# Where DVE adds the kept shared-expert output to the residual in a mixture-of-experts layer

## The chip, the cores and the metric

The kernel runs on one core of a Trainium2 chip. The metric is the time of one launch in device microseconds; smaller is better. Times given here are a median of several runs, and a profile is one execution of its own, recorded by the hardware.

## The reference, cut to what matters

The reference is a stack of four layers on x of 4 sequences x 1024 tokens x 128 features, in float32. Each layer has an attention-like part and a feed-forward part, with a layer norm behind each. The change lies in the feed-forward part of the last layer, a mixture of 32 experts of width 128, of which each token uses 4, and a shared expert of width 512 that every token uses:

```python
def _L3_ffn_ref(x, ...):
    flat = x.reshape(B * T, D)
    scores = softmax(flat @ router_w.T + router_bias)
    topk_scores, topk_idx = top_k(scores, 4)
    topk_scores = topk_scores / clip(topk_scores.sum(-1), 1e-12)
    h = silu(einsum('nd,ehd->neh', flat, gate_w)) * einsum('nd,ehd->neh', flat, up_w)
    expert_out = einsum('neh,edh->ned', h, down_w)
    sel = take_along_axis(expert_out, topk_idx[:, :, None], axis=1)
    out = (sel * topk_scores[:, :, None]).sum(axis=1)
    out = out + silu(flat @ sgate_w.T) * (flat @ sup_w.T) @ sdown_w.T
    return out.reshape(B, T, D)
...
x = layernorm(x + _L3_attn_ref(x, ...))
x = layernorm(x + _L3_ffn_ref(x, ...))
```

The layer's first part, `_L3_attn_ref`, forms u and v (256 wide) from the normalised rows, mixes v between tokens with a Toeplitz matrix per head, multiplies by u and projects back to 128.

## The kernel before

The residual x stays in SBUF for the whole kernel, as 32 tiles of 128 tokens x 128 features. Layer 3 takes the tokens in three parts: a (the first half, 16 tiles), b and c (a quarter each, 8 tiles, so 128 x 1024 numbers). Each part passes these steps:

- `l3_attn` (L1561): the attention-like part. For each of two halves of the width PE and ACT make v and u (L1626, L1580), and DVE mixes v with the Toeplitz weights and multiplies by u (L1637, L1639, L1643; 4 + 12 + 4 instructions a half).
- `l3_route`: the router; DVE selects four experts of each token and computes for each (token, choice) its place in a list sorted by expert, `posl3b` for part b.
- `spread`: POOL scatters the rows of x with indirect DMAs into that list in DRAM, `l3rb`, 8 x 4 = 32 DMAs of 128 rows (L1301).
- `l3_shared` (L1686): the shared expert. PE, ACT (L739) and DVE (`hs`, L740) make it; for parts b and c the result is not added at once but kept by ACT in an SBUF tile `sh`, since the spread still reads x as it was.
- `small_experts` (L1718), called for this layer by `l3_experts`: SP loads the list in groups of 512 rows (`xg`, L1332), PE transposes them (`tp`, copied to `xgT` by ACT, L167), multiplies by the gate and up weights of the experts (`gu`, L157), ACT applies silu (`sg`, L1748), DVE multiplies (`hg`, L1749), PE turns that round and DVE copies it out (`hT`, L169), PE multiplies by the down weights, ACT copies the result (`yg`), and SP writes it to a second list in DRAM, `l3yb`. In step g the code emits `up(g + 1)`, `turn(g)` (the one with `hT`), `inputs(g + 2)` and `down(g - 1)`; the last step, g == ng, holds only the last `down`, and then `rest_of`, an If for lists that are longer than expected, which is not taken here.
- `collect` (L1381): POOL gathers the rows back (`yt`, L1301), and DVE adds each with its weight to x (L1392). There are eight buffers for `yt`, so POOL's later gathers wait for DVE's adds.
- `finish` or `close`: the last norm (L192 to L209) and SP's DMAs to the output (`out_x`, L1808).

`all` weaves these together. A generator `on` holds the side work in order: part b's spread and part a's collect and finish abreast of part c's `l3_attn` and route, then c's spread, then b's collect and finish. `mix` lets the side work advance beside the main work (shared expert and experts of b, then of c) by the estimated durations that the steps yield. The order on each engine is then settled when the program is built: a planner takes the instructions by estimated times, within their dependencies, and an instruction may so be placed far from where it is written. `queued` is what ties side work down: every instruction that the side generator emits gets an ordering edge (without a semaphore) behind the last instruction that the main work has emitted on the same engine, which `self.latest` holds.

The line of this change stands in the loop over b and c:

```python
self.run(self.mix(self.l3_experts(p, wall3), on, 0.75, p is c))
s = slice(p.t0, p.t0 + QT)
self.nc.vector.tensor_tensor(self.x[:, s, :], sh, self.x[:, s, :], ALU.add)
```

It is written behind the experts (L1962), and does not go through `queued`, so it has its data dependencies alone: `sh` must be there, and the part's spread must have read x.

Of the kernel before, what the change touches and what calls it, by code (L numbers as in the profile page):

```python
# [15 lines left out]
ALU = mybir.AluOpType  # L16
# [14 lines left out]
QT = NT // NQT  # L31
# [11 lines left out]
E3, F3, K3 = 32, 128, 4  # L43
# [31 lines left out]
class Kernel:  # L75
# [1585 lines left out]
    def l3_route(self, part):  # L1661
        nc = self.nc
        with ExitStack() as ctx:
# [15 lines left out]
            yield from self.positions(cp, "l3" + part.name, mask, w, part.nt, E3, K3)  # L1679
            yield (10.0,)  # L1680

    def mark(self, name):
        self.listed.add(name)
        yield (0.0,)
# [30 lines left out]
        cp = self.pool(ctx, "l1fw")  # L1715
        return self.load(cp, self.ins["l1_w"])

    def small_experts(self, lay, ne, part, wall):  # L1718

        nc = self.nc  # L1720
        pos, wk, ids, done, used = self.route[lay + part.name]
        rows, ys, total = self.lists[lay, part.name]
        tl = self.likely(part, ne, K3)
        with ExitStack() as ctx:
            gp = self.pool(ctx, lay + "fg" + part.name, 3)
            ps = self.pool(ctx, lay + "fpe" + part.name, 2, space=PSUM)
            ng = tl // 4
            xgTs, ess, hs, hTs = {}, {}, {}, {}

            def inputs(g):  # L1730
                xg = self.gathered(gp, rows, g, done, part.nt * K3)
                xgTs[g] = self.tile(gp, [P, BLK], "xgT")
                self.transposes(ps, xgTs[g], [xg[:, i, :] for i in range(4)], on_act=True, tag="tp")

            def up(g):
                es = ess[g] = self.experts_of(ids, g, ne)
                xgT = xgTs.pop(g)
                h = hs[g] = self.tile(gp, [P, 4, P], "hg")
                for c in range(2):
                    pg = self.tile(ps, [P, 2, 2, P], "gu")  # L1740
                    for i in range(2):
                        self.mm(
                            pg[:, i].rearrange("p a f -> p (a f)"),
                            xgT[:, (2 * c + i) * P : (2 * c + i + 1) * P],
                            wall[:, bass.ds(es[2 * c + i] * (3 * P), 2 * P)],
                        )
                    sg = self.tile(gp, [P, 2, P], "sg")
                    nc.scalar.activation(sg, pg[:, :, 0, :], AF.Silu)  # L1748
                    nc.vector.tensor_tensor(h[:, 2 * c : 2 * c + 2, :], sg, pg[:, :, 1, :], ALU.mult)  # L1749

            def turn(g):
                h = hs.pop(g)
                hT = hTs[g] = self.tile(gp, [P, BLK], "hT")
                self.transposes(ps, hT, [h[:, i, :] for i in range(4)], on_act=False, tag="tp")

            def down(g):
                es, hT = ess.pop(g), hTs.pop(g)
                py = self.tile(ps, [P, 4, D], "yp")
                for i in range(4):
                    pm = self.mm(py[:, i, :], hT[:, i * P : (i + 1) * P], wall[:, bass.ds(es[i] * (3 * P) + 2 * P, P)])  # L1760
                yg = self.tile(gp, [P, 4, D], "yg")
                if lay == "l3" or g % 2:
                    nc.scalar.copy(yg, py)
                    marks = (pm,)
                else:
                    marks = (pm, nc.vector.tensor_copy(yg, py))
                nc.sync.dma_start(
                    out=ys[g * 4 * P : (g + 1) * 4 * P, :].rearrange("(t p) d -> p t d", p=P), in_=yg
                )
                return marks  # L1770

            def rest(g):
                inputs(g)
                up(g)
                turn(g)
                down(g)


            inputs(0)
            inputs(1)  # L1780
            up(0)
            for g in range(ng + 1):
                if g + 1 < ng:
                    up(g + 1)
                if g < ng:
                    turn(g)
                if g + 2 < ng:
                    inputs(g + 2)
                marks = down(g - 1) if g else ()
                if g == ng:  # L1790
                    self.rest_of(used, tl, total, rest)
                    self.listed.add(f"made {lay}{part.name}")
                yield (3.7, *marks)
# [1 line left out]
    def l1_experts(self, part, wall):  # L1795
        return self.small_experts("l1", E1, part, wall)

    def l3_experts(self, part, wall):
        return self.small_experts("l3", E3, part, wall)

    def finish(self, part):

# [84 lines left out]
    def all(self):  # L1887
        a, rest = self.first, self.rest
        b, c = rest
        r = self.both[1]  # L1890
        a2, m2, n2 = self.by_rows
        with ExitStack() as ctx:
            lgp = self.pool(ctx, "l2lg")
            self.l2_lg = self.tile(lgp, [P, NT, E2], "lg")
            with ExitStack() as early:
# [13 lines left out]
                with ExitStack() as c2:  # L1909
                    wall = self.l1_wall(c2)  # L1910
# [4 lines left out]
            with ExitStack() as c2:  # L1915
                wall = self.l1_wall(c2)
# [6 lines left out]
            on = self.served(  # L1923
                self.chain(self.rows_in(a2), self.onward(a, True)),
                (lambda: self.rows_done >= B + 2, self.routed(m2)),
                (lambda: self.rows_done == 2 * B, self.routed(n2)),
            )
            self.run(self.mix(self.l2_attn(1), on, drain=False))
            with ExitStack() as c3:
                with ExitStack() as c2:  # L1930
                    wall = self.l2_wall(c2)
                    self.press(on, listed("l2m"))
                    self.run(self.mix(self.l2_experts(m2, wall), on, drain=False))
                    self.press(on, lambda: {"l2n", "routed l3a"} <= self.listed)
                    sw, wall3 = self.l3_wall(c3, True)
                    on = self.chain(on, self.rows_in(m2))
                    self.run(self.mix(self.l2_experts(n2, wall), on, drain=False))
                self.press(on, listed("l3a"))
                yp = self.pool(c3, "l3y", 8)

                on = self.chain(
                    on, self.collect("l2", n2, K2, yp, which=(0, 1, 4, 5)),
                    self.abreast(
                        self.chain(self.l3_attn(b), self.mark("mixed l3b"), self.l3_route(b)),
                        self.collect("l2", n2, K2, yp, which=(2, 3, 6, 7)),
                    ),
                    self.abreast(
                        self.chain(self.spread("l3", b, K3), self.when(listed("made l3a")), self.last(a, yp)),
                        self.chain(self.l3_attn(c), self.mark("mixed l3c"), self.l3_route(c)),
                    ),  # L1950
                    self.spread("l3", c, K3), self.when(listed("made l3b")), self.last(b, yp),
                )
                self.run(self.mix(self.chain(self.l3_shared(a, sw), self.l3_experts(a, wall3)), on, 0.75, False))
                hold = self.pool(c3, "l3hold", 2)
                for p in (b, c):
                    self.press(on, listed("mixed l3" + p.name))
                    sh = self.tile(hold, [P, QT, D], "sh")
                    self.run(self.mix(self.l3_shared(p, sw, sh), on, 0.75, False))
                    self.press(on, listed("l3" + p.name))
                    self.run(self.mix(self.l3_experts(p, wall3), on, 0.75, p is c))  # L1960
                    s = slice(p.t0, p.t0 + QT)
                    self.nc.vector.tensor_tensor(self.x[:, s, :], sh, self.x[:, s, :], ALU.add)  # L1962
                self.run(self.close(c, yp))
        bad = self.nc.values_load(self.flag[0:1, 0:1], min_val=0, max_val=1)
        with self.tc.If(bad > 0):
            with ExitStack() as ctx:
# [9 lines left out]
                for p in self.parts:  # L1976
                    self.run(self.onward(p))
                    with ExitStack() as c2:
                        sw, wall = self.l3_wall(c2)
# [167 lines left out]
```

## Time and profile before

| | |
|---|---|
| time, median of 3 runs | 2411.06 us (2410.7 to 2413.85) |
| profiled execution | 2413.21 us, of it 2411.4 us span |
| mean granted TensorE clock | 0.818 of full speed |
| busy: PE, DVE, ACT, POOL | 1616.9, 1263.6, 825.0, 722.6 us |
| part b: spread on POOL | 2047.03 to 2088.3 us |
| part b: experts on PE, first and last `hT` on DVE | 2092.67 us on; 2121.99 and 2194.61 us |
| part c: spread on POOL | 2225.00 to 2270.3 us |
| part c: last `hT` on DVE | 2350.97 us |
| part c: gathers on POOL | 2357.50 to 2386 us |
| the adds of `sh` (L1962) | 2 x 1.226 us, at 2089.66 and 2271.62 us |

Times in the profile are microseconds from the start of the span. A line of a timeline gives the start, the duration, engine, line of the code, operation, output <- inputs, how many instructions are put together, and in brackets the engine's idle time just before, with what ended it. `DMA l3rb<-x,posl3b` is the scatter of part b, `yt<-l3ya,posl3a` a gather of part a. "issue" is time in which the engine waited for nothing that the profile shows.

### The profile page before, as it was taken

To read this page: it belongs to the slowest core of one execution; us is meant where nothing else is said; L and a number is where in the kernel's file an instruction comes from. 1 tells how busy PE (TensorE), PEld (TensorE's weight loads), DVE (VectorE), ACT (ScalarE), POOL (GpSimd) and SP (SyncE) were. 2 spreads that over 40 slices of the span, in tenths; PEclk is the share of its full clock that TensorE was granted. 3 is DMA by queue.
4 is the path that set the end of the run, shared out by engine and by line. 5 is a ranking of instruction groups with operands and counts; after the bars stand their busy time and mean duration, and the time that the engine had idled before them with its cause. 6 is when DMAs were issued, how large, how long until landed. Compare 5 with 4: busy or idle time off the path is not lost. (4 is left out here: it accounts for less than half of the span.)

```text
span 2411.4 us, 27036 instructions
## 1 busy us (share of the span) xinstructions
PE 1616.9 (67%) x9017; PEld 967.3 (40%) x9017; DVE 1263.6 (52%) x3630; ACT 825.0 (34%) x1180; POOL 722.6 (30%) x681
## 2 busy tenths in 40 slices
PE   7626876975661778487969787887745798357160
PEld 3214333853320337345623232344523486245160
DVE  8957894655570565224545675473611265236233
ACT  6701571422330333122236564642201164223030
POOL 1031484135227000435132002002272200735725
PEclk9856887988785888788979998988977899678575
DMA  9930002334101016212130000031321131222232
GB/s 309 288 112 0 20 34 90 112 115 160 62 31 53 15 34 200 83 44 74 38 106 21 1 1 16 3 114 40 143 85 35 44 112 46 76 79 62 89 89 68
DMA packets 215530, 187.10 MB, mean 78 GB/s; under 512 B 16528, under 2 KB 194064, under 8 KB 214864
## 3 DMA queue, kind: packets, MB, share of 16 engines
q1 hardware_dynamic: 194672, 142.29, 18.7%
q0 software_dynamic: 20704, 42.86, 5.8%
q8 instruction: 84, 1.38, 0.2%
q14 instruction: 70, 0.57, 0.1%
HBM read 88.49 MB, written 96.60 MB: 77 GB/s over the span
## 5 line engine op out<-in xcount | busy, mean ns | idle before, releaser
L1055 ACT ACTIVATE pr<-sc 128x1024 f32<-128x1024 f32 x288 | 279.7, 1021 | 319.9 <-PE sc L157 184.9
L157 PE MATMUL gu<-ld,xgT 128*128 x640 | 177.4, 423 | 88.8 <-issue 38.7
L157 PE MATMUL sc<-qm,kT 32*128 32x512 f32 (+3 forms) x1536 | 199.2, 558 | 13.7 <-issue 12.3
L157 PE MATMUL s<-pr,va 128*32 128x512 f32 (+3 forms) x1536 | 177.1, 528 | 46.0 <-issue 26.2
L157 PEld LDWEIGHTS gu<-ld,xgT 128*128 128x128 f32 x640 | 127.5, 210 | 119.1 <-issue 49.7
L165 PE MATMUL tp<-ld,hg 128*128 128x128 f32 x624 | 104.0, 289 | 92.1 <-ACT hT L167 38.0
L169 DVE COPY hT<-tp 128x512 f32<-128x512 f32 x118 | 81.0, 686 | 159.3 <-remote 73.9
L157 PE MATMUL gu<-wall,xgT 128*128 x304 | 156.1, 640 | 2.7 <-ACT xgT L167 2.0
L1061 DVE TENSOR_TENSOR pr<-pr,ld 128x512 f32<-128x512 f32 (+1 forms) x160 | 92.2, 581 | 100.6 <-ACT pr L1055 98.5
L165 PEld LDWEIGHTS tp<-ld,hg 128*128 128x128 f32 x624 | 81.5, 149 | 144.7 <-issue 46.9
L165 PE MATMUL tp<-ld,xg 128*128 128x128 f32 x396 | 68.9, 305 | 102.1 <-DMA xg<-l3rc 48.5
L1749 DVE TENSOR_TENSOR hg<-sg,gu 128x256 f32<-128x256 f32 x160 | 65.8, 417 | 134.9 <-ACT sg L1748 95.8
L167 ACT COPY xgT<-tp 128x512 f32<-128x512 f32 x99 | 58.0, 586 | 213.0 <-PE tp L165 91.1
L157 PEld LDWEIGHTS sc<-qm,kT 32*128 32x128 f32 x1536 | 84.8, 197 | 113.6 <-issue 77.4
L1507 ACT ACTIVATE sg<-gu 128x512 f32<-128x512 f32 x76 | 45.2, 597 | 225.7 <-PE gu L157 109.4
L1748 ACT ACTIVATE sg<-gu 128x256 f32<-128x256 f32 x160 | 61.1, 385 | 163.2 <-PE gu L157 80.9
L1301 POOL DMA_INDIRECT l1ra<-x,posl1a x64 | 93.1, 1455 | 59.5 <-DVE posl1a L1276 40.3
L157 PEld LDWEIGHTS s<-pr,va 128*32 128x32 f32 x1536 | 38.9, 113 | 156.6 <-issue 109.5
L1509 DVE TENSOR_TENSOR hg<-sg,gu 128x512 f32<-128x512 f32 x76 | 51.7, 682 | 92.1 <-ACT sg L1507 48.7
L1301 POOL DMA_INDIRECT yt<-l1yr,posl1r x64 | 60.9, 951 | 124.1 <-DVE x L1392 79.3
L165 PEld LDWEIGHTS tp<-ld,xg 128*128 128x128 f32 x396 | 52.4, 158 | 107.6 <-issue 59.0
L1301 POOL DMA_INDIRECT l1rr<-x,posl1r x64 | 61.7, 965 | 99.5 <-DVE posl1r L1276 80.3
(440 smaller groups left out, 3498.8 us busy)
## 6 DMA issues: line engine op xcount, KB each, us to landing
wall<-wall SPq DMA_DIRECT2D x16, 768.0 KB
l3ra<-zero SPq DMA_DIRECT2D x1, 6144.0 KB
ld<-in_l_w SPq DMA_DIRECT2D x2, 3072.0 KB
wall<-we SPq DMA_DIRECT2D x24, 256.0 KB
ld<-in_l_w SPq DMA_DIRECT2D x1, 6144.0 KB
l1ra<-zero SPq DMA_DIRECT2D x1, 5120.0 KB
l1rr<-zero SPq DMA_DIRECT2D x1, 5120.0 KB
xg<-l3ra SPq DMA_DIRECT2D x20, 256.0 KB
```

Of the source, the lines that this page charges most:

```text
L157: return self.nc.tensor.matmul(out, lhsT, rhs, start=start, stop=stop)
L165: nc.tensor.transpose(pt[:, k * P : (k + 1) * P], s, self.ident)
L167: nc.scalar.copy(dst, pt[:, : n * P])
L169: nc.vector.tensor_copy(dst, pt[:, : n * P])
L1055: nc.scalar.activation(pr, sc[h], AF.Exp)
L1061: nc.vector.tensor_tensor(d, d, cst["tril"].unsqueeze(1).unsqueeze(1).to_broadcast([P, 2, n, P]), ALU.mult)
L1301: ins = self.nc.gpsimd.indirect_dma_start(**kw)
L1507: nc.scalar.activation(sg, gu[:, 0, :], AF.Silu)
L1509: nc.vector.tensor_tensor(h, sg, gu[:, 1, :], ALU.mult)
L1748: nc.scalar.activation(sg, pg[:, :, 0, :], AF.Silu)
L1749: nc.vector.tensor_tensor(h[:, 2 * c : 2 * c + 2, :], sg, pg[:, :, 1, :], ALU.mult)
```

## The change

The add becomes a small generator, `held`, that is handed to the experts. In their last step, behind the last `turn` and ahead of the If, `queued` emits it, so that it gets the ordering edge behind DVE's last instruction of the main work, the last `hT` copy. The line behind the experts in `all` goes. The add itself, its operands and its duration stay the same; it is done once for b and once for c.

```diff
+    def held(self, part, sh):
+
+        s = slice(part.t0, part.t0 + part.nt)
+        self.nc.vector.tensor_tensor(self.x[:, s, :], sh, self.x[:, s, :], ALU.add)
+        yield (1.0,)
+
...
-    def small_experts(self, lay, ne, part, wall):
+    def small_experts(self, lay, ne, part, wall, held=None):
...
                 if g == ng:
+                    if held:
+                        self.queued(held)
                     self.rest_of(used, tl, total, rest)
...
-    def l3_experts(self, part, wall):
-        return self.small_experts("l3", E3, part, wall)
+    def l3_experts(self, part, wall, held=None):
+        return self.small_experts("l3", E3, part, wall, held)
...
-                    self.run(self.mix(self.l3_experts(p, wall3), on, 0.75, p is c))
-                    s = slice(p.t0, p.t0 + QT)
-                    self.nc.vector.tensor_tensor(self.x[:, s, :], sh, self.x[:, s, :], ALU.add)
+                    self.run(self.mix(self.l3_experts(p, wall3, self.held(p, sh)), on, 0.75, p is c))
```

## The prediction

> **What bounds the kernel now.** I read the page first (section 1: PE busy 67% of the span, DVE 52%, POOL 30%, so no engine carries the whole), then the one line that the change moves, then the timelines of DVE, POOL and PE around it, and last a table of busy time by stretch. The source view of L1962 gives the two adds, what DVE stood for ahead of them, and that nothing is listed as having waited for them:
>
> ```profile
> L1962 DVE TENSOR_TENSOR x<-sh,x x2: 1226/1226/1226, 2089.7 to 2271.6; 128x1024 f32<-128x1024 f32 x2
> ...
>   DMA l3rc<-x,posl3c: 33.7, 1
>   DMA l3rb<-x,posl3b: 30.5, 1
> ```
>
> So the adds do not run where the program writes them, behind the experts. They need `sh` and the end of the spread (the scatters read the rows of x that the add overwrites), and DVE takes them as soon as it may: part b's at 2089.66, part c's at 2271.62, each time ahead of the experts' first `hg`. DVE is in order, so what stands behind them waits too. DVE's timeline shows what that is for b:
>
> ```profile
> 2089.66 1.23 DVE L1962 TENSOR_TENSOR x<-sh,x 128x1024 f32<-128x1024 f32 x1 [30.54 <-DMA l3rb<-x,posl3b]
> 2090.80 0.61 DVE L1637 TENSOR_SCALAR y<-v,ld 128x256 f32<-128x256 f32 x2
> 2091.32 2.46 DVE L1639 SCALAR_TENSOR_TENSOR y<-v,ld,y 128x256 f32<-128x256 f32 x6
> ...
> 2098.75 0.42 DVE L1749 TENSOR_TENSOR hg<-sg,gu 128x256 f32<-128x256 f32 x1 [0.73 <-ACT sg L1748]
> ...
> 2120.10 0.35 DVE L1392 SCALAR_TENSOR_TENSOR x<-yt,wkl3a,x 128x128 f32<-128x128 f32 x1 [15.81 <-DMA yt<-l3ya,posl3a]
> ```
>
> Half of part c's Toeplitz mix (2090.80 to 2098.03, 7.2 us) lies behind the add, with its inputs ready since 2066.1, when ACT ended the last u. The first `hg` is not held by it: it waits for ACT's sg. And PE, ahead of both, waited for the same spread:
>
> ```profile
> 2092.67 2.01 PE L165 MATMUL tp<-ld,xg 128*128 128x128 f32 x8 [26.25 <-DMA xg<-l3rb]
> ```
>
> POOL's timeline is what sets these stretches: 32 scatters of b from 2047.03 at 1.27 us each, then at once the gathers of part a. Its indirect DMAs take about 0.95 us, but not beside the add and the Toeplitz mix, nor beside a long run of L1392:
>
> ```profile
> 2088.62 0.98 POOL L1301 DMA_INDIRECT yt<-l3ya,posl3a  x1 [0.30 <-issue]
> 2089.91 1.81 POOL L1301 DMA_INDIRECT yt<-l3ya,posl3a  x1 [0.30 <-issue]
> 2092.03 0.99 POOL L1301 DMA_INDIRECT yt<-l3ya,posl3a  x1 [0.30 <-issue]
> 2093.32 1.95 POOL L1301 DMA_INDIRECT yt<-l3ya,posl3a  x1 [0.30 <-issue]
> 2095.58 2.93 POOL L1301 DMA_INDIRECT yt<-l3ya,posl3a  x1 [0.31 <-issue]
> ...
> 2226.33 5.98 POOL L1301 DMA_INDIRECT l3rc<-x,posl3c  x1 [0.30 <-issue]
> ...
> 2271.87 1.82 POOL L1301 DMA_INDIRECT yt<-l3yb,posl3b  x1 [0.30 <-issue]
> ```
>
> The table by stretch shows the stages (the columns are PE, PEld, DVE, ACT and POOL busy, then granted clock, DMA share, GB/s): while POOL works without a break, PE hardly does, behind the spread too (12.61 of 41 us), and it is full only once the gathers have stopped.
>
> ```profile
> 2047.00:2088.00 41.00, 12.24 (x45) 6.90 (x45) 10.10 (x41) 10.66 (x19) 31.53 (x32) 0.67 0.16 59
> 2104.00:2145.00 41.00, 12.61 (x38) 8.48 (x37) 5.41 (x14) 4.88 (x9) 25.37 (x27) 0.62 0.21 56
> 2145.00:2197.00 52.00, 46.63 (x288) 41.05 (x288) 34.47 (x124) 26.76 (x52) 10.20 (x11) 0.89 0.31 91
> ```
>
> **The change, part by part.** Durations are those of the profiled execution, 2413.21 us (span 2411.4 and 1.8 around it); the median of the runs is 2411.06, so 2.15 comes off at the end.
>
> *The two stands go (30.54 and 33.70 us of DVE).* Worth nothing by themselves: the spread hides them. PE's next work waited 26.25 us for xg of the same spread, and 48.52 us in part c. If that cover were gone they would cost the whole 64 us.
>
> *The Toeplitz half moves* to about 2066, beside the scatters. Out of the gathers it takes 1.95 + 2.93 - 2 x 0.95 = 2.98 us of POOL. Beside scatters the price lies between 0 (the eight L209 at 2235.68, beside which the scatters of 2235.14 and 2236.41 stayed at 0.96) and 4.3 (32 of L1392, the same operation as L1639, cost one scatter 5.98 - 0.96 = 5.02 in 8.48 us of DVE; for 7.2 us that is 4.3). I take 2.98, the same instructions beside the same engine. So 0 for POOL's stream as a whole, with -2.98 to +1.3 as ends; the experts of b may start up to 4.3 later.
>
> *The adds leave the gathers:* -(1.81 - 0.95) - (1.82 - 0.95) = -1.73 us of POOL. Both streams then end sooner by that, and what PE gets behind them with it.
>
> The Trainium skill ("SBUF — State Buffer", section "Who interferes with whom") says that a tensor_tensor with both inputs in SBUF contends only with GpSimd's reads, and infers that writing descriptors escapes it; by that rule the adds cost POOL nothing and the sum would be 0 in place of -1.73. The two rows of 1.81 and 1.82 us speak against the rule here.
>
> *The eight L209 behind c's add* (2272.77, 2.23 us) move to about 2238, and SP's four out_x DMAs behind them to the same place, away from between the loads of xg on SP's queue. Nothing on either side (0 to -1): the third xg is used only at 2282.20.
>
> *b's add in its new place.* DVE's last hT of b ends at 2195.28; the add then takes 1.23 ahead of six L1392 and the route of c (posl3c at 2202.97). Behind that, DVE has 2.38 us idle ahead of `hs` (2205.53), waiting for PE, and POOL reaches the spread of c only at 2225.00. So 0; with that cover gone, +1.23, and POOL's gather beside it could take 0.86 more. Ends: 0 and +2.1.
>
> *c's add in its new place*, at about 2351.65 behind the last hT. Behind it wait four L1392, statistics, the DVE branch of the If (2355.9) and the L209 of part b. The last gathers start at 2357.50; the chain of waits names L209 for that, but these write b's rows, which a gather of l3yc doesn't use; SP passed the If only at 2356.8, after the last l3yc write had landed. DVE then idles 2.21 us for the first yt. So 0; if DVE does gate the gathers, +1.23.
>
> Sum: -1.73, between -5.7 and +2.9 (-1.73 with -2.98 and -1, or with +1.3, +2.1 and +1.23). 2413.21 - 1.73 - 2.15 = 2409.3.
>
> **The rivals.** *A wait that takes the place of the one removed (slower).* DVE's order is planned, and the add's place is free in it. At 2104.30 DVE already stood 15.81 us for a gather of part a (L1392), with `hg` behind it. If such an L1392 now comes ahead of the experts' first `hg` rather than behind the third, that `hg` slips from 2098.75 to about 2118. The price is at least the 5.5 us of experts' work that was done from 2098.75 to 2104.30, at most the whole 15.81 again; I take 10, which gives 2419. It decides as soon as one L1392 precedes the first `hg`. For it: this order is a matter of a microsecond in the plan. Against: the trace shows three `hg` going first.
>
> *The freed DVE time carries through (faster).* POOL stood 52.5 us in four waits for DVE's L1392 of part a (33.59, 11.24, 2.24, 5.38), and so c's spread began at 2225.00, 22.0 after posl3c was ready. If 7.2 us less DVE work among the experts of b brings those adds forward by as much, the spread and all behind it come 7.2 + 1.7 = 8.9 earlier, at most 22 + 1.7 = 23.7; I take 11, which gives 2400. Against it: DVE had time enough from 2104 to 2143, and it was PE and ACT that stood.
>
> *The add stays where it was.* The edit ties it behind the last hT on DVE, so hardly: 2411.
>
> **How the numbers follow.** 0.2% is 4.8 us, about what a measurement of this kernel can tell from no change (its runs lie 3.2 apart): faster is below 2406.2, slower above 2415.9. The sum's case: 0.42 (0.09 faster, 0.29 same, 0.04 slower, as the order elsewhere may shift a little); its own range is 2405 to 2414. The carry-through: 0.28 (0.27 and 0.01 same). The new wait: 0.27 (0.26 and 0.01 same). The add unmoved: 0.03, same. Together 0.36 faster, 0.34 same, 0.30 slower. The range runs from 2393 (half way from 2400 to its end of 2387) to 2422 (half way from 2419 to its end of 2409.3 + 15.8 = 2425), which leaves out about one in ten on each side.
>
> **What would show it.** Right: no DVE idle of 30 us ahead of an add; the Toeplitz half at about 2066 to 2073; part a's second to fifth gather at 0.95; scatters of 1 to 4 us beside the mix; both adds right behind the last hT, with DVE idle behind them. Wrong: an L1392 ahead of the first `hg`; spread c starting before 2220 or after 2230; gathers of c starting over 1 us after SP has passed the If; or the order of PE and ACT in the experts of b differing from before.

## The result, and the profile after

The changed kernel takes 2408.92 us (median of 11 runs, 2402.6 to 2417.2); the kernel before, over 11 runs, 2413.85 us (2410.1 to 2419.7). The ratio is 0.9979, with a 95% interval of 0.9964 to 0.9995: a gain of 0.05 to 0.36%, against 2409.3 us, or 0.07% below 2411.06, that were forecast. The profiled execution took 2410.17 us, with a span of 2408.4.

DVE's timeline after the change, to be read against the one shown before: the Toeplitz half now runs at 2060, as soon as the first v is there, and the adds run 2.4 and 3.5 us behind the last hT copy of their part.

```profile
2060.35 0.61 DVE L1637 TENSOR_SCALAR y<-v,ld 128x256 f32<-128x256 f32 x2 [3.10 <-issue]
...
2096.27 0.42 DVE L1755 TENSOR_TENSOR hg<-sg,gu 128x256 f32<-128x256 f32 x1 [28.49 <-ACT sg L1754]
...
2115.47 0.35 DVE L1392 SCALAR_TENSOR_TENSOR x<-yt,wkl3a,x 128x128 f32<-128x128 f32 x1 [15.59 <-DMA yt<-l3ya,posl3a]
...
2192.99 1.15 DVE L1685 TENSOR_TENSOR x<-sh,x 128x1024 f32<-128x1024 f32 x1
...
2200.11 0.69 DVE L740 TENSOR_TENSOR hs<-sg,pu 128x512 f32<-128x512 f32 x1 [1.86 <-PE pu L157]
...
2232.65 2.14 DVE L209 TENSOR_SCALAR x<-x,mv,rstd 128x128 f32<-128x128 f32 x8
...
2352.01 1.19 DVE L1685 TENSOR_TENSOR x<-sh,x 128x1024 f32<-128x1024 f32 x1
...
2356.80 0.35 DVE L1392 SCALAR_TENSOR_TENSOR x<-yt,wkl3c,x 128x128 f32<-128x128 f32 x1 [2.71 <-DMA yt<-l3yc,posl3c]
```

DVE's stand has not gone; it has only changed its name. It lasts 28.49 us and ends with ACT's sg, and the second one of 15 us, for a gather of part a, is there as before. PE waits for the same load as before:

```profile
2091.96 1.97 PE L165 MATMUL tp<-ld,xg 128*128 128x128 f32 x8 [27.38 <-DMA xg<-l3rb]
```

What changed is POOL's timeline. Scatters beside the mix are longer than 0.96 us, the first gathers of a and b are short, the gather beside the moved add of b is long (1.64 us), and one scatter of c is longer than it was (7.33 us; 5.98 before):

```profile
2061.44 1.15 POOL L1301 DMA_INDIRECT l3rb<-x,posl3b  x1 [0.30 <-issue]
...
2067.05 1.56 POOL L1301 DMA_INDIRECT l3rb<-x,posl3b  x1 [0.30 <-issue]
...
2089.14 0.97 POOL L1301 DMA_INDIRECT yt<-l3ya,posl3a  x1 [0.30 <-issue]
2090.41 0.94 POOL L1301 DMA_INDIRECT yt<-l3ya,posl3a  x1 [0.30 <-issue]
...
2193.32 1.64 POOL L1301 DMA_INDIRECT yt<-l3ya,posl3a  x1 [0.30 <-issue]
...
2219.67 7.33 POOL L1301 DMA_INDIRECT l3rc<-x,posl3c  x1 [0.31 <-issue]
...
2267.76 0.97 POOL L1301 DMA_INDIRECT yt<-l3yb,posl3b  x1 [0.30 <-issue]
```

The long scatter is not the change's doing: two later profiles of the same two kernels have it the other way round, 7.33 us before and 5.98 after. In each of these four profiles it ends about 0.86 us after DVE's run of 32 adds of part a, and either the first or the second scatter of c is the one that is caught, which moves the spread of c by 1.2 us. The longest scatter beside the mix varies in the same way, with 1.56 us here and 3.00 us in the later profile of this kernel.

The second place where something changed is SP's queue at the start of part c's experts. First before the change, then after it:

```profile
2271.67 0.92 SPq L1332 DMA_DIRECT2D xg<-l3rc  x2
2273.39 2.01 SPq L1808 DMA_DIRECT2D out_x<-x  x4
2275.45 1.77 SPq L1332 DMA_DIRECT2D xg<-l3rc  x3
```

```profile
2267.56 0.37 SPq L1332 DMA_DIRECT2D xg<-l3rc  x1
2268.02 2.18 SPq L1816 DMA_DIRECT2D out_x<-x  x4
2270.25 2.00 SPq L1332 DMA_DIRECT2D xg<-l3rc  x3
```

The four output DMAs of part a stood behind the second load of xg; now they stand behind the first, and the second load comes 2.70 us behind the first in place of 0.42. The table by stretch (part b's experts; columns as before) shows the same two regimes as before the change:

```profile
2102.00:2143.00 41.00, 10.39 (x35) 7.71 (x36) 6.16 (x15) 5.01 (x10) 23.27 (x25) 0.64 0.23 61
2143.00:2195.00 52.00, 44.10 (x285) 38.97 (x283) 35.68 (x127) 26.93 (x52) 12.49 (x12) 0.92 0.32 91
```

Put together from POOL's timelines, in us. The last two columns are the same two kernels on another chip, number 4 of the record. The experiments ran on this one and on chips 2 and 15. On these three the kernel before has medians of 2053 to 2055 us, and its runs lie between 2043 and 2063 us, apart from two slow ones on chip 4 (4570 and 8117 us):

| stage | before | after | before, chip 4 | after, chip 4 |
|---|---|---|---|---|
| spread of b | 41.3 | 42.4 | 41.2 | 43.7 |
| first 36 gathers of a | 48.7 | 44.7 | 49.7 | 46.3 |
| first scatter of b to first scatter of c | 178.0 | 174.5 | 155.0 | 153.9 |
| spread of c | 45.3 | 46.5 | 46.5 | 45.3 |
| gathers of b | 40.6 | 39.7 | 40.8 | 39.8 |
| last gather of b to first gather of c | 46.3 | 48.0 | 15.3 | 18.6 |
| first gather of c to the end | 53.9 | 54.1 | 53.9 | 53.9 |
| first scatter of b to the end | 364.4 | 363.2 | 311.7 | 311.7 |

Of the 3.0 us between the two first spans, 1.9 had arisen before the first scatter of b (2047.03 against 2045.17), where the order on PE, DVE, ACT and POOL is the same; the part that the change touches gives 1.2. (The gathers of c before the change last to 2397.3 us, not to 2386 as said above.)

### The profile page after: what moved, and what is told of

It is laid out like the page before. It is cut to its first block, busy times and chain, and to the rows that moved or that the text cites. A ratio compares the mean times of both kernels' runs of the same rounds, so it can differ in the third digit from the quotient of the medians.

```text
span 2408.4 us, 27028 instructions
## 1 busy us (share of the span) xinstructions
PE 1599.0 (66%) x9017; PEld 956.7 (40%) x9017; DVE 1262.4 (52%) x3630; ACT 822.5 (34%) x1179; POOL 720.1 (30%) x681
## 5 line engine op out<-in xcount | busy, mean ns | idle before, releaser
L157 PE MATMUL gu<-wall,xgT 128*128 x304 | 155.0, 636 | 2.7 <-ACT xgT L167 2.0
L1301 POOL DMA_INDIRECT l1ra<-x,posl1a x64 | 93.0, 1454 | 59.0 <-DVE posl1a L1276 39.8
```

Source lines behind the costliest of these rows:

```text
L157: return self.nc.tensor.matmul(out, lhsT, rhs, start=start, stop=stop)
L1301: ins = self.nc.gpsimd.indirect_dma_start(**kw)
```

## The experiments

The theory: the change works through what DVE runs beside POOL's indirect DMAs; DVE's stand itself is worth nothing; and SP's order gives back in part c what POOL saves. The rivals: the add alone hindered POOL, the order elsewhere did it, or DVE's stand cost time. Of the stages in the table, two differ between the first chip and chip 4: 23 us up to c's spread and 31 between the gathers of b and of c, much of it on the first chip in waits that its profile names "remote" (ended by something that it cannot name) and "issue". Why is not known, so the experiments are compared with one another and with the two kernels on chip 4. A profile's stages repeat better than the times, but not exactly. With c's add in the same place, the gathers of b repeat to 0.2 us. But in kernels with the same order on DVE and POOL in part b, the spread of b takes 42.4 or 43.7 us, and the 36 gathers end between 88.2 and 90.2 us from its first scatter; a difference of 1 us there between two profiles shows nothing by itself.

**Both kernels on chip 4.**

> The kernel before, unchanged, for its profile on the same chip as the next three. On the chip of the first four runs the kernel before took 2053 us and not 2411, and engines stood less for 'remote' and 'issue'. Theory: first scatter of b to the end of the first 36 gathers of a 91.3 us, as in only_c, which has the same order up to there; gathers of b 40.8; first xg load of c to the first hT of c 10.7 us, as in only_b.

> The changed kernel, unchanged, on that chip. Theory (POOL saves, SP gives back): first scatter of b to the end of the first 36 gathers 90.2 us, about 1 less than before; gathers of b 39.8, 1 less; but SP now holds four out_x DMAs between the first and the second xg load of c, so first xg load to first hT of c takes 12.7 to 15.6 us, 2 to 5 more than before. Sum within 3 us of before, so the ratio lies between 0.9985 and 1.0015. Rival (POOL alone): 10.7 us there too, and 2 us faster.

Measured: 91.25 and 90.24 us from the first scatter of b to the end of the 36 gathers, gathers of b 40.8 and 39.8, first xg load of c to first hT 11.4 and 13.6, to the last hT 48.5 and 50.7. Ratios: 0.9997 (0.9976 to 1.0017) and 0.9988 (0.9969 to 1.0006). The two savings of 1 us and the loss of over 2 are all there; neither ratio is clear of 1.

**One add at a time** (chip 2). In `all`:

```diff
-self.l3_experts(p, wall3, self.held(p, sh))
+self.l3_experts(p, wall3, self.held(p, sh) if p is b else None)   # only_b; only_c: p is c
+... behind the experts, for the other part: self.run(self.held(p, sh))
```

> Part b's add moved as in the change, part c's left where it was. Theory (POOL): the change works only through what DVE runs beside POOL's gathers. From the first scatter of b to the end of the first 36 gathers of a: 87.4 us as in the changed kernel (90.3 before); the gathers of b take 40.6 us as before (39.7 in the changed kernel). Time about 0.9 us above the changed kernel's, 1 to 3 below before. Rival (order): what the planner reorders elsewhere carries the difference; then part c alone, whose order of loads and transposes changes, carries it, and this kernel is equal to before within 1 us.

> Part c's add moved as in the change, part b's left where it was. Theory (POOL): first scatter of b to the end of the first 36 gathers of a 90.3 us as before, DVE idle 30 us ahead of the add of b; gathers of b 39.7 us as in the changed kernel; time 0 to 1 us below before. If the end of those gathers to the first gather of c still takes 48.0 us (46.3 before), c's move costs as much behind them as it saves. Rival (order): most of the gain is here, 2 us or more below before.

only_b: 90.16 us to the end of the 36 gathers (87.4 was expected from the first chip), gathers of b 40.8, first load to first hT 10.7; ratio 0.9999 (0.9976 to 1.0021). only_c: 91.25, 39.75, but 15.6 to the first hT, and 22.5 us from the gathers of b to those of c; ratio 1.0015 (0.999 to 1.0041). From the first scatter of b to the end: 311.5 and 316.3 (311.7 before). So in the profile c's move alone costs more than it brings (the ratio leaves that open), and nothing there speaks for the rival by which it would carry the gain. The gains in time that were expected, 1 to 3 us and 0 to 1 us, don't show in these ratios.

**The mix parted from the add** (chip 2). mix_first ties b's early add behind the mix; stand_kept keeps the wait, in one column's multiplication by 1, but not the add:

```diff
+add_manual_dep(add.ins, <last L1643 of the first half>, NoSync)      # mix_first
...
+e = self.x[:, p.t0 + QT - 1, 0:1]                                    # stand_kept, for b
+self.nc.vector.tensor_scalar(e, e, 1.0, None, ALU.mult)
```

> Part b's add stays ahead of the experts and waits for the spread, but is tied behind part c's first half of the Toeplitz mix; part c's add as in the change. It parts the mix from the add. Theory (POOL): the spread of b takes 42.4 us as in the changed kernel, the first 36 gathers of a 44.7 + 0.9 = 45.6 (48.7 before), their sum ends at 88.3 us from the first scatter. The stand of DVE ahead of the add is about 21 us, and hides nothing. Rival (the stand itself costs): the run ends at 90 as before.

> The changed kernel with one more DVE instruction, a multiplication by 1 of one column of the last tile of part b's x, that waits for the spread of b where the add did, ahead of the Toeplitz mix: the stand is kept, the 1.2 us of the add beside the gathers are not. Theory (POOL): DVE idle about 30 us ahead of it; the spread of b takes 41.3 us as before, the first 36 gathers of a 48.7 - 0.9 = 47.8, their end 89.4 us from the first scatter; time about 2 us above the changed kernel's. Rival (only the add hindered POOL, the mix doesn't): 87.4 us as in the changed kernel, and the same time.

POOL's timeline in mix_first, a scatter beside the mix and the gather beside the add; then DVE's stand and the gather beside the mix in stand_kept:

```profile
1760.45 3.00 POOL L1301 DMA_INDIRECT l3rb<-x,posl3b  x1 [0.31 <-issue]
...
1785.25 1.82 POOL L1301 DMA_INDIRECT yt<-l3ya,posl3a  x1 [0.30 <-issue]
```

```profile
1783.70 0.15 DVE L1970 TENSOR_SCALAR x<-x 128x1 f32<-128x1 f32 x1 [30.49 <-DMA l3rb<-x,posl3b]
```

```profile
1788.55 3.27 POOL L1301 DMA_INDIRECT yt<-l3ya,posl3a  x1 [0.30 <-issue]
```

To the end of the 36 gathers, all on chip 2: 90.10 (mix moved), 90.75 (add moved), 90.16 (both, only_b), 91.25 (neither, only_c). The spread takes 43.6 us with the mix beside it and 41.2 without. So both hinder POOL, wherever they run. What each move is worth alone these sums don't show, since 90.10 to 90.75 lies within what the stage varies by. With neither moved it ended at 91.25 both times (only_c, before_here), and with both at 88.2 to 90.2, so together they bring 1 to 3 us, though ACT's order at the start of b's experts differs between these kernels too. The whole stand of 30.49 us, put back, costs 0.35 us to the end (312.07 against 311.72 in the changed kernel on chip 4), less than such stages vary: it is hidden. Ratios 0.9992 and 1.0006, neither clear of 1. The 88.3 and 89.4 expected were too low by 1.4 to 1.8: the spread took 43.6 us and not 42.4 in mix_first, and in both kernels the second half of the mix runs beside these gathers on this chip and lengthens two or three of them (1.09 to 1.95 us).

**SP's order** (chip 15). Part a's output DMAs from ACT's queue:

```diff
-self.nc.sync.dma_start(
+(self.nc.scalar if part is self.first else self.nc.sync).dma_start(
```

> The changed kernel, but part a's eight output DMAs are issued by ACT and not by SP, so that none stands between two loads of xg; DVE and POOL keep their order, PE and ACT take the second transposes of xg ahead of the experts' first products again, as before the change. Theory (the DMAs on SP's queue give back what POOL saves in part c): the second xg load is issued 0.4 us behind the first (2.7 in the changed kernel), first load to first hT of c 10.7 to 11.5 us (13.6), from the last gather of b to the first of c 16.3 us (18.6), gathers of b stay at 39.8; from the first scatter of b to the end 309.5 us (311.7), time 1 to 3 us below the changed kernel's. Rival (the load's delay is hidden, the order of PE and ACT made the difference or nothing did): 13 us or more from first load to first hT, and the same time.

The second load comes 0.41 us behind the first, first load to first hT 12.0 (13.6 with the DMAs between the loads), last gather of b to first gather of c 16.7 (18.6), from the first scatter to the end 308.6, 3.1 below. Of these 3.1 us, 2.0 lie behind the gathers of b; the others arose ahead of c's spread, which the DMAs don't touch. The place is shown by all the kernels with eight buffers on these chips: first load to first hT takes 12.7 to 15.6 us where the DMAs stand between the loads, and 10.7 to 12.0 where they don't. Between out_on_act and the changed kernel the order on PE and ACT differs too (the second transposes of xg ahead of the first products or behind them), and no run parts that from the DMAs. The time does not show it: 0.9995 (0.9977 to 1.0013).

**What the new places have to spare** (chip 15). Three more adds of zeros behind each moved add:

> The changed kernel with three more DVE instructions of the same size behind each of the two moved adds (x plus zeros), about 3.5 us more at each place. It asks what the new places cost when they are no longer covered. Theory: in part b 1.9 us of DVE's idle time ahead of hs take half of it, the rest is seen by at most 2 us in the start of c's spread; in part c the gathers start where they did, as they don't wait for DVE, and DVE has 2.7 us idle for the first yt; from the first scatter of b to the end 311.7 to 314 us. Rival (DVE gates the spread and the gathers at both places): 7 us more, 318.7.

To the end 313.9 us (311.7), 1.0001 (0.9978 to 1.0024). In part b the extra adds are hardly seen: c's spread starts 154.2 us behind the first scatter of b (153.9). In part c only the moved add stands ahead of the If; the planner put the three extra ones behind it:

```profile
1990.24 1.19 DVE L1686 TENSOR_TENSOR x<-sh,x 128x1024 f32<-128x1024 f32 x1
...
1991.67 2.45 DVE L1688 TENSOR_TENSOR x<-zero,x 128x1024 f32<-128x1024 f32 x2
...
1994.16 1.23 DVE L1688 TENSOR_TENSOR x<-zero,x 128x1024 f32<-128x1024 f32 x1
...
1997.35 0.34 DVE L1392 SCALAR_TENSOR_TENSOR x<-yt,wkl3c,x 128x128 f32<-128x128 f32 x1
```

The first gather started at 1992.72, while DVE was still adding, so these gathers don't wait for DVE's work behind the If, though the chain of waits names it (L209). What they do wait for is in the traces: in all fourteen profiles the first gather of c starts 0.97 us after the last write to `l3yc` has landed (1991.75 and 1992.72 here, 2356.53 and 2357.50 before the change, 2353.26 and 2354.23 after it). In out_on_act and stand_kept the moved add ended 0.1 us after that landing, and the gather was no later. More DVE work ahead of the If was not tried. Of the 2.2 us to the end, 1.1 arose ahead of the adds of c (first load to first hT 14.7 us against 13.6); in part c the norm behind the extra adds held the first add of gathered rows to 1997.35, 1.8 us after its yt had landed.

**Dense DVE work beside the scatters** (chip 4). The largest hindrance in these traces is neither add nor mix, but the last 32 adds of part a, 8.5 us without a gap beside c's first scatters. In spaced and spaced_b the order on every engine stays that of the changed kernel and of only_b, and those adds only wait:

```diff
+behind = done[len(done) - 3 if n == 0 else len(done) - 1]   # 2nd or 4th scatter of c's tile
+add_manual_dep(<first L1392 of the tile>, behind, Sync)
```

> The changed kernel with its instructions in the same order on every engine, but the last 32 adds of part a (L1392), which DVE ran without a gap beside the first scatters of c, now wait in groups of four for the second and the fourth scatter of each of c's first four tiles. Theory (dense DVE work holds POOL): the spread of c takes 41.2 to 42.5 us in place of 46.5, and all behind it comes about 4 us earlier, time 2 to 5 us below the changed kernel's. Rival (the long scatter has another cause, the start of the spread itself): 46.5 us and the same time.

> As the last, but only part b's add is moved; part c's stays where it was before the change. Theory: the spread of c 41.2 to 42.5 us, first xg load to first hT of c 10.7 us since the out_x DMAs stay behind the second load, gathers of b 40.8; 1 to 4 us below the last kernel, 4 to 8 below before. Rival (the order of SP doesn't matter): 12.7 us or more there, and 1 us above the last kernel for the slower gathers.

```profile
1906.53 1.92 DVE L1903 SCALAR_TENSOR_TENSOR x<-yt,wkl3a,x 128x128 f32<-128x128 f32 x7 [2.19 <-DMA l3rc<-x,posl3c]
```

With such gaps, at most seven adds in a row, no scatter of c takes over 1.01 us, and the spread takes 40.4 us in place of 45.3 to 46.5. To the end: 307.5 and 305.5 us (311.7). Times 2047.23 and 2045.34 us; ratios to the kernel before 0.9975 (0.9955 to 0.9995) and 0.9962 (0.9941 to 0.9984). spaced_b, with c's add left early, has its first hT 11.5 us behind the first load, spaced 14.1.

**More buffers for yt** (chip 15), sixteen in place of eight on top of spaced_b; yt16_act adds c's move and the output DMAs on ACT:

```diff
-yp = self.pool(c3, "l3y", 8)
+yp = self.pool(c3, "l3y", 16)
```

> spaced_b with sixteen buffers for yt in place of eight, so that POOL gathers the whole of part a without a wait for DVE's adds; all 64 adds of a then wait for scatters of c, four at a time. Theory (what starts c's spread is POOL's stand for DVE's adds of part a, and not the route, which is ready 18 us sooner): c's spread starts when posl3c is ready, about 136 us from the first scatter of b (154 in spaced_b), and from the first scatter of b to the end it takes 288 to 292 us (305.5); time 12 to 18 us below spaced_b. Rival (something else in c, the shared expert or the experts of b, holds the start): 300 us or more.

> The last kernel with the change in full (part c's add moved too) and part a's output DMAs on ACT. Theory: gathers of b 39.8 us where the last has 40.6, no DMA between the loads of xg; within 2 us of the last kernel, as ACT now waits for part a's norm ahead of some of its copies. Rival (ACT is held by these DMAs): 3 us or more above the last kernel.

yt16_b takes 2019.22 us, a ratio of 0.9833 (0.9802 to 0.9865); yt16_act 2026.56 us, 0.9863 (0.9835 to 0.9892). The second is 7 us behind in time, as its rival said, but in the profile's stages level (282.4 us to the end in yt16_b, 281.3 in yt16_act). The profile of yt16_b is of an execution of 2031.42 us, 12 us above its median, so that stays unsettled. yt16_b moved more than expected, and the expectation named but half of the cause. DVE's timeline at the start of b's experts, in spaced_b and then in yt16_b:

```profile
1813.50 0.35 DVE L1397 SCALAR_TENSOR_TENSOR x<-yt,wkl3a,x 128x128 f32<-128x128 f32 x1 [17.09 <-DMA yt<-l3ya,posl3a]
```

```profile
1801.58 0.42 DVE L1763 TENSOR_TENSOR hg<-sg,gu 128x256 f32<-128x256 f32 x1 [0.78 <-ACT sg L1762]
1801.92 0.68 DVE L169 COPY hT<-tp 128x512 f32<-128x512 f32 x1
```

With eight buffers an add of part a stands among the first `hg` and waits 17 us for its gather; with sixteen all these adds come later, and the first hT of b is there 54.7 us after the first scatter, not 73.4. POOL also gathers without a stand, and c's spread starts at 123.9 us (154.0), as soon as POOL has done the 64 gathers; posl3c was ready 10 us sooner. What each of the two is worth alone, no run shows. First load to first hT of c gives 6 us back (17.4 against 11.5).

## Why the prediction was right

*The stands are worth nothing*: right, by stand_kept. *The new places are covered*: right, for b by heavy and in the trace (1.86 us idle behind the add, ahead of hs), for c by the trace, where the last write to `l3yc` and not DVE releases the gathers (2.71 us idle behind the add). The add of b holds a gather in its new place too, 1.64 us in place of 0.95; POOL's next stand, 4.24 us in place of 5.38, hides that. The adds do not stand right behind the last hT, as was said, but 2.4 and 3.5 us behind it.

*The Toeplitz mix*: mis-sized. Out of the gathers it took about 3 us, as said; beside the scatters it cost 1.1 us in some profiles (the first chip's, out_on_act and the two with sixteen buffers) and 2.4 in the others, in place of 2.98, so the move brought a gain of its own. It started at 2060 and not at 2066, since it needs v first and u last. *The add of b*, 0.86: one gather was longer by 0.87 where the add stood, but what was left of that behind the 36 gathers, 0.5 us by stand_kept and nothing by mix_first against only_b, is less than the stage varies by. *The add of c*, 0.87: 0.9 and 1.0.

*The L209 and SP's DMAs behind c's add*, "nothing on either side (0 to -1)": wrong, in sign. L209 went to 2232, but the DMAs did not move with it into the spread: on SP's queue they stand behind the first load of xg and were issued at 2268.02, though their rows were ready at 2234.8; so they moved ahead of the second load. That is 1.6 to 2.0 us by out_on_act, together with the order of PE and ACT that goes with it, and eats the saving of part c.

*The sum* of -1.73 thus came out as -1.2 on the first chip and 0.0 on chip 4, with the mix's gain left out and one term of the wrong sign. In both, c's long scatter, which falls either way without the change, has its part: +1.2 on the first chip, -1.2 on chip 4. Without it the stages give about -2.4 and +1.2, so even the sign is not settled by them. The measured ratio of 0.9979 and chip 4's 0.9988 (0.9969 to 1.0006) both leave room for the sum; that the median fell by 4.9 is more than the stages show, and the rest was not traced to the change. That 2408.92 lies 0.4 us from the 2409.3 forecast is luck: the forecast started from 2411.06, the median of three runs, while eleven runs of the same kernel gave 2413.85.

The Trainium skill ("SBUF — State Buffer", section "Who interferes with whom") infers that a tensor_tensor doesn't hinder the writing of descriptors. In mix_first, where nothing else ran on DVE beside it, the add still made one gather 1.82 us long in place of 0.95. The same section says that a DVE instruction with two SBUF inputs contends with a GpSimd instruction that reads SBUF, and these DMAs do take their row numbers from an SBUF tile; that agrees, but no run here separates reading from writing.

*The rivals.* The new wait did not arise: the first three `hg` still go before the first L1392. But the wait itself was in both kernels, and yt16_b shows what it costs together with POOL's stands. The carry-through did not come either: POOL's first stand for part a's adds lasted 33.63 us (33.59 before). The buffers are one cause of it, by yt16_b; PE and ACT, which the prediction named, were not tested. Two of the signs named for a wrong prediction did appear: c's spread started at 2219.67, below 2220, of which 1.9 us lie ahead of the change; and ACT's order in the experts of b changed (its next v now precedes the first sg).

## What to carry to other kernels

An engine's long stand is worth something only if what stands behind it is what someone waits for; here PE and ACT waited for the same spread, and the stand ran beside it. When an instruction is moved, read the order of every queue that its neighbours feed: SP's DMAs went ahead of a load and, in the profiles, took back the gain. Where POOL issues indirect DMAs, break up dense VectorE work (0.25% in spaced), and give a gather enough buffers that neither engine waits for the other (1.7% in yt16_b, with those gaps). When a chain of waits names an engine, check over several profiles which event the start follows at a constant distance.

## What the runs showed of the hardware

An indirect DMA on POOL takes 0.95 us with VectorE idle, and up to 7.3 us beside VectorE work without a gap; the one that is caught ends about 0.86 us after the run of adds does. Not every one is caught: a gather at 2223.75 in the kernel before took 0.95 us beside the same run, and in yt16_b a run of sixteen adds (4.43 us) held no scatter (1.03 us at most). The same 32 adds with gaps after at most seven cost it nothing (1.01 at most). And the same kernel took 2414 us on one chip and 2053 to 2055 on three others. In the profiles 304 us of that lie ahead of part b's spread; in the two later stages that were compared, much of it is in stalls that the profile names "remote" and "issue". The cause stays open.
